# Sums of k v applied head by head, the tokens' root one list later, queries ahead of the last values, the last tile's layers in line

## The chip, the cores and the metric

The kernel runs on one core of one Trainium2 chip. The metric is the device time of one execution in microseconds (us), lower being better. Two kernels are compared by the medians of their runs. A profiled execution is one further execution, taken with the hardware profiler; its trace is what the profile's views are read from.

## What is computed

An input `x` of 256 channels by 64 by 64 positions (all float32) passes through two layers.

```python
# layer 0: x + conv(groupnorm(x)); 8 heads of 32 channels, each pixel a token
q, k = sigmoid(Wq x), sigmoid(Wk x);  v = (Wv x) / norm(v)
Ik  = integral(k)                      # running sums over rows and columns
Ikv = integral(k v^T)                  # a 32x32 matrix per head and pixel
for w in (1, 2, 4):                    # windows of 64, 32 and 16 pixels a side
    attn = q . box(Ikv, 64 // w)
    norm = q . box(Ik, 64 // w)
    outs.append(attn / (norm + 1e-6))
x = x + Wout concat(outs) + bout
# layer 1: 4096 tokens of 256
t = t + attention_ffn(layernorm(t))    # causal softmax, masked scores filled with -32767
t = t + experts(layernorm(t))          # top 2 of 8 experts, chosen once for all tokens
```

## The kernel before

It runs in three stages, one after the other on the same core: `window_attention` (to about 1031 us of the trace), `causal_attention` (to about 1771) and `experts`. TensorE (PE in the profile) does all products; its results land in PSUM and are evacuated by ScalarE (ACT) or VectorE (DVE). GpSimd is POOL, and SP and the other queues issue DMAs.

**The window stage.** `window_heads` runs twice, once for each half of the heads (hg = 0 and 1), so each call has four heads of 32 channels on the 128 partitions. Sums over a window are not taken from an integral image of `k v` at each pixel. They are split: keys near the window's edge are handled as masked scores (`push`: a mask product L348 and a score product L357 for each head, an evacuation with a maximum at zero L326 or L328, then `add`: the product with the values L390), and whole blocks of 8x8 pixels through `ikv`, the integral over blocks of the 32x32 sums of k v. For a row block Y (8 pixel rows) and each of the two smaller windows (`wi` = 1, 2), `states(Y)` forms with VectorE the 32x32 sums of the blocks that lie wholly inside (`srows` L487, `st8` L490 to L495) and spreads each into four block-diagonal matrices `bd`, one per head, in which the rows of the other heads are zero (eight copies on ScalarE, L498). `inside` then multiplies `bd` with `q` into the accumulator: for each of the 8 column blocks X and each head one product over all 128 partitions, L409. A float32 product shows as two matmul records.

Parts are packed into lists of up to 512 columns, and a loop over Y and over the lists i of Y (from L664) interleaves the rest: `spread_norms` at i = 1 (product L473, copies `rn` L476), the boxes of `ik` for the next Y on GpSimd at i = 2 (L440 to L453), the output product `convolve(Y - 1)` at i = 3 (L507, added to `t` at L512), and for hg = 1 `causal.norm(Y - 1)` at i = 4 and `causal.turn(Y - 1)` at i = 7. `norm` takes the statistics of four token tiles (L704, L705), the root of their variance (L709 on ScalarE) and its reciprocal (L710), and writes the four normalised tiles `xn` (L837); `turn` transposes them (L846). At Y = 7, `causal.load` puts the weights of attention into the memory of the integral image `ik`; three small buffers, `after`, `sums` and `count`, come from the same piece of memory.

**The order of the work.** In the window stage the orders of PE and POOL are written by hand: they follow the program's text. The orders of DVE, ACT and the DMA queues are made when the program is built, by a planner that forecasts when each instruction becomes ready; the program's text gives priorities. In `causal_attention` only PE's order is by hand. On each engine instructions run strictly in the order so made, and an instruction that waits holds all behind it.

**The attention stage.** The 32 query tiles of 128 tokens are taken from the last down, the 20 large ones (31 to 12) in turn, with the 12 small ones in between. `queries(g)` makes the queries of four tiles (L916, evacuated at L918), `scores` L956 with evacuation L958, row maximum L964 and exponential L969; `attend` transposes the weights (L986, copies `sT` L989) and multiplies with the values (L1000); `finish` L1010 to L1012. `causal.values(g)` makes four tiles of values (L856, evacuated at L858). Since masked scores count with a finite fill, the tokens behind a tile enter through `behind()`: running sums of `xs` (`sums`, filled first at L924, then 31 additions L926) times the value weights (L931), stored in `after` (L933). When four tiles are finished, `layers` queues six steps on the list `later`: first (L1040), turn (L1048, L1049), hidden (L1057, L1059), last (L1067 to L1075), norm (L1082), turn_again (L1090, L1091); `one()` takes one step from the list. The last group (tiles 12 to 15) does this for tiles 13 to 15 and then for tile 12 alone. `experts` begins with sums over all tokens, which need the last `turn_again`.

Of the kernel before, what the change touches and what calls it, by code (L numbers as in the profile page):

```python
# [177 lines left out]
def window_attention(tc, a, t, eps5, ident, causal, first):  # L178
# [5 lines left out]
    with ExitStack() as ctx:  # L184
# [99 lines left out]
        with tc.manual_schedule(engines={mybir.EngineType.PE}):  # L284
            causal.values(0, psum)
            for f in late:
                f()
            xns = causal.norm(7, w)
            causal.values(1, psum)
            causal.values(2, psum)  # L290
            causal.turn(7, xns, psum)


def window_heads(tc, a, t, ident, hg, norm, raws, load, psum, pools, tables, consts, late, causal):
# [109 lines left out]
    def inside(group, acc):  # L404

        wi, Y = group
        for X in range(8):
            for h, hs in enumerate(hss):
                nc.tensor.matmul(  # L409
                    acc.rearrange("p (y x) -> p y x", x=HW)[hs, :, 8 * X : 8 * X + 8],  # L410
                    lhsT=state["bd"][wi][:, X, h, :], rhs=q[:, 8 * Y : 8 * Y + 8, 8 * X : 8 * X + 8],
                    start=(X == 0), stop=False, skip_group_check=True,
                )

# [65 lines left out]
    def states(Y):  # L480


        out = [None]
        for wi in (1, 2):
            n = HALF[wi] // 8
            rows = state["h"].tile([P, 9, 32], F32, name="srows")
            nc.vector.tensor_sub(rows, ikv[:, min(8, Y + n), :, :], ikv[:, max(0, Y - n + 1), :, :])  # L487
            st = state["h"].tile([P, 8, 32], F32, name="st8")
            if n == 2:
                nc.vector.tensor_copy(st[:, 0, :], rows[:, 2, :])  # L490
                nc.vector.tensor_sub(st[:, 1:7, :], rows[:, 3:9, :], rows[:, 0:6, :])
                nc.vector.tensor_sub(st[:, 7, :], rows[:, 8, :], rows[:, 6, :])
            else:
                nc.vector.tensor_copy(st[:, 0:4, :], rows[:, 4:8, :])
                nc.vector.tensor_sub(st[:, 4:8, :], rows[:, 8:9, :].to_broadcast([P, 4, 32]), rows[:, 1:5, :])  # L495
            bd = state["h"].tile([P, 8, 4, 32], F32, name=f"bd{wi}")
            for h in range(4):
                nc.scalar.activation(bd[:, :, h, :], st, AF.Copy, scale=heads[:, 32 * h : 32 * h + 1])  # L498
            out.append(bd)
        return out  # L500

    def convolve(Y):
# [89 lines left out]
    with tc.manual_schedule(engines={mybir.EngineType.PE, mybir.EngineType.Pool}), ExitStack() as keys:  # L592
# [72 lines left out]
        for Y in range(8):  # L665
            ov = [None]
            for wi in (1, 2):
                o = h.tile([P, 8, HW], F32, name=f"ov{wi}")
                nc.sync.dma_start(out=o, in_=oscratch[wi].rearrange("b p (y x) -> y p b x", x=HW)[Y])
                ov.append(o)  # L670
            bd = states(Y)
            if hg and Y == 7:
                causal.load()
            for i, parts in enumerate(lists[Y]):
                if (Y, i) != (0, 0):
                    push(parts)
                if i == 2 and Y < 7:
                    boxed = boxes(Y + 1)
                if i == 1:
                    state.update(bd=bd, ov=ov, rn=spread_norms(r))  # L680
                if i == 3 and Y:
                    convolve(Y - 1)
                if hg and i == 4 and Y:
                    xns = causal.norm(Y - 1, w)
                if hg and i == 7 and Y:
                    causal.turn(Y - 1, xns, psum)
                if i == len(lists[Y]) - 3 and Y < 7:
                    r = norms(boxed)
# [87 lines left out]
class Causal:  # L776
# [23 lines left out]
    def load(self):  # L800
        nc, a = self.nc, self.a
        w = self.iks.tile([P, (HW + 1) * (HW + 1)], F32, name="ik")
        at = [0]

        def take(shape):
            n = int(np.prod(shape[1:]))
            s = w[0 : shape[0], at[0] : at[0] + n]
            at[0] += n
            return s.rearrange("p (c e) -> p c e", c=shape[1]) if len(shape) == 3 else s

        self.mm, self.mb, self.wvu, self.bvc = (take(d.shape) for d in self.fold)
        for i in (2, 3, 0, 1):
            nc.sync.dma_start(out=(self.mm, self.mb, self.wvu, self.bvc)[i], in_=self.fold[i])
        self.wt, self.col, self.row = {}, {}, {}
        for name in ("b1", "g_ln", "beta_ln"):
            s = self.col[name] = take([P, DC])
            nc.sync.dma_start(out=s, in_=a["L1_" + name].rearrange("(c p) -> p c", p=P))
        for name in ("W1", "W2"):
            s = self.wt[name] = take([P, DC, D])
            nc.sync.dma_start(out=s, in_=a["L1_" + name].rearrange("(c p) e -> p c e", p=P))  # L820
        for name in ("L1_b2", "L1_g_lnff", "L1_beta_lnff", "gamma", "beta"):
            s = self.row[name.removeprefix("L1_")] = take([P, D])
            nc.sync.dma_start(out=s, in_=a[name].partition_broadcast(P))
        self.after = take([NT, D + 1])
        self.sums = take([P, DC, NT])
        self.count = take([NT, 1])

    def norm(self, g, pool):
        nc = self.nc
        for i in range(4 * g, 4 * g + 4):  # L830
            statistics(nc, self.low, self.t[:, i, :], self.stats[:, i, :])
        rsqrt(nc, self.stats[:, 4 * g : 4 * g + 4, 1], self.eps5)
        xns = []
        for i, tag in enumerate(("l0Wq", "l0Wk", "l0Wv", "l0bo")):
# [26 lines left out]
class Given:  # L861
# [3 lines left out]
    def __init__(self, nc, a, pool, causal):  # L865
        def tile(name, shape, src=None):
            s = pool.tile(shape, F32, name=name)
            if src is not None:
# [14 lines left out]
        nc.gpsimd.memset(self.before, 1.0)  # L883
        nc.gpsimd.affine_select(out=self.before, in_=self.before, compare_op=ALU.is_gt, fill=0.0, base=0,
                                pattern=[[1, NE], [-1, NE]], channel_multiplier=0)
        self.stats = tile("stats2", [P, NT, 2])
        self.sums = tile("sums2", [P, DC, NQ + 1])
        self.parts = 0
# [2 lines left out]
def causal_attention(tc, t, ident, eps5, causal, big, given):  # L891
# [4 lines left out]
    with ExitStack() as ctx:  # L896
# [1 line left out]
        ps = ctx.enter_context(tc.tile_pool(name="l1ps", bufs=2, space=PSUM, reuse_waits="tile"))  # L898

        causal.rest(big)  # L900
        x, v, stats, after = causal.x, causal.v, causal.stats, causal.after
        mm, mb, wt, col, row = causal.mm, causal.mb, causal.wt, causal.col, causal.row
        x2 = {}
        for g in range(NQ):
# [15 lines left out]

        def behind():

            sums, count = causal.sums, causal.count
            nc.vector.memset(sums[:, :, NT - 1 :], 0.0)  # L924
            for i in reversed(range(NT - 1)):
                nc.vector.tensor_add(sums[:, :, i : i + 1], sums[:, :, i + 1 : i + 2], causal.xs[:, :, i + 1 : i + 2])  # L926
# [171 lines left out]
        with tc.manual_schedule(engines={mybir.EngineType.PE}):  # L1098
# [5 lines left out]
            def need(i):  # L1104
                if i // 4 not in qTs:
                    qTs[i // 4] = queries(i // 4)
# [3 lines left out]
                    later.pop(0)()  # L1110

            causal.values(3, value_psum)
            causal.values(7, value_psum)
            need(larges[0])
            for at, part in enumerate(scores(larges[0])):
                part()
                if at < 3:
# [3 lines left out]
            for r, i in enumerate(larges):  # L1121
# [7 lines left out]
                if r + 1 < len(larges):  # L1129
                    need(larges[r + 1])  # L1130
                    parts = scores(larges[r + 1])
                    for part in parts[:-1]:
                        part()
                    one()
                    todo.pop(0)()
                    parts[-1]()
                half = len(todo) // 2
                for step in todo[:half]:
                    step()
# [186 lines left out]
```

## Time and profile before

| | us |
|---|---|
| three runs | 2015.45, 2017.11, 2014.27 |
| median | 2015.45 |
| the profiled execution | 2017.58 |
| its span in the trace | 2015.9 |
| mean granted clock of PE | 0.977 of full speed |
| PE busy | 1862.9 |
| DVE, ACT, POOL busy | 985.5, 829.0, 431.2 |

The page's first part gives busy time, share of the span and the number of instructions for each engine; "PEld" is the loading of weights, which overlaps PE. A line of the timeline reads: start, duration, engine, source line, operation, what it writes `<-` what it reads, partitions and elements, how many instructions are merged in it, and in brackets the idle time of the engine before it and what ended that wait. In a line of a group by tile, the numbers behind the colon are the shortest, median and longest duration in ns, then the first and last start in us. A line under "who waited" is the idle time in us and the number of waits. In a table by stretches, a line reads: the stretch, its length, the busy time and the number of instructions of PE, PEld, DVE, ACT and POOL, then the granted clock of PE, the DMA share and the traffic in GB/s.

### The profile page before, as it was taken

How to read it: one execution, taken by the hardware profiler on the slowest of the kernel's cores; microseconds unless marked ns; L12 is line 12 of the kernel's file. 1: busy time of each engine (PE TensorE's matmuls, PEld its weight loads, DVE VectorE, ACT ScalarE, POOL GpSimd, SP SyncE). 2: the span in 40 equal slices, each digit the busy share in tenths (PEclk: the TensorE clock that was granted, in tenths of full speed). 3: DMA queues.
4: the chain of work that ended last, by engine and by line, in shares of the span. 5: the costliest groups of instructions: out<-in, count | busy, mean ns of one | idle time of the engine just before them, and what ended most of it. 6: DMA issues, size and time to landing. Idle time of an engine off the chain costs nothing.

```text
span 2015.9 us, 46364 instructions
## 1 busy us (share of the span) xinstructions
PE 1862.9 (92%) x20326; PEld 1224.0 (61%) x20326; DVE 985.5 (49%) x2190; ACT 829.0 (41%) x1459; POOL 431.2 (21%) x709
## 2 busy tenths in 40 slices
PE   4999899999999999898899999999999999879998
PEld 2655565555665565555574765666666666547787
DVE  4644444544554465555463434554554555433343
ACT  0566555554356654554413323332333233223322
POOL 1384322232155122333110000000000000021220
PEclk9999999999999999999999999999999999979999
DMA  7211000000331100000200000000000000010000
GB/s 239 80 52 50 23 13 16 15 18 13 96 98 40 44 18 13 18 13 12 49 2 0 0 1 0 1 1 0 1 0 1 0 1 0 1 42 21 21 21 21
DMA packets 66891, 53.35 MB, mean 26 GB/s; under 512 B 37568, under 2 KB 56792, under 8 KB 66688
## 3 DMA queue, kind: packets, MB, share of 16 engines
q1 hardware_dynamic: 57296, 31.87, 5.8%
q10 hardware_dynamic: 8128, 14.67, 2.1%
q0 software_dynamic: 1264, 3.84, 0.6%
q8 instruction: 159, 2.61, 0.5%
q14 instruction: 44, 0.36, 0.1%
HBM read 32.93 MB, written 17.44 MB: 25 GB/s over the span
## 4 chain that ended last, share of the span: by engine, by line
PE 42%; DVE 6%; ACT 3%; issue 2%; POOL 0%; ACTq 0%; DVEq 0%; POOLq 0%
PE po L1000 11%; PE pa L956 9%; PE ph L1260 6%; PE py L1280 5%; PE pt L986 2%; PE pm L1057 1%; PE acc L390 1%; PE pm L1067 1%; PE ps L357 1%; PE ps L507 1%; DVE lnst L704 1%; DVE sT L989 1%; DVE nbs L964 1%; PE pm L916 1%; ACT s L969 1%
## 5 line engine op out<-in xcount | busy, mean ns | idle before, releaser
L326 ACT ACTIVATE pm<-ps 128x512 f32<-128x512 f32 (+19 forms) x734 | 362.6, 559 | 320.3 <-issue 164.9
L328 DVE TENSOR_SCALAR pm<-ps 128x512 f32<-128x512 f32 (+23 forms) x442 | 267.8, 636 | 291.6 <-PE ps L357 210.8
L390 PE MATMUL acc<-pm,vh 128*32 128x248 f32 (+22 forms) x3424 | 220.1, 359 | 19.8 <-DVE pm L328 19.6
L357 PE MATMUL ps<-q,kh 32*128 32x248 f32 (+23 forms) x3424 | 209.8, 360 | 0.0
L956 PE MATMUL pa<-k,qT 128*128 128x512 f32 (+3 forms) x416 | 180.2, 574 | 7.1 <-ACT qT L918 5.7
L348 PE MATMUL ps<-table,table 32*128 32x192 bf16 (+19 forms) x2512 | 146.1, 262 | 39.3 <-DVE pm L328 18.4
L989 DVE COPY sT<-pt 128x512 f32<-128x512 f32 (+3 forms) x144 | 92.7, 643 | 138.1 <-PE pt L986 137.9
L348 PEld LDWEIGHTS <-table 32*128 32x128 bf16 x2512 | 51.0, 92 | 179.7 <-issue 172.8
L390 PEld LDWEIGHTS acc<-pm,vh 128*32 128x32 f32 x3424 | 88.9, 111 | 110.3 <-issue 63.2
L357 PEld LDWEIGHTS ps<-q,kh 32*128 32x128 f32 x3424 | 146.2, 192 | 7.5 <-issue 2.7
L425 POOL TENSOR_TENSOR y<-y,rn 128x512 f32<-128x512 f32 x32 | 40.8, 1275 | 477.5 <-DVE y L424 335.0
L958 ACT ACTIVATE s<-pa,v 128x512 f32<-128x512 f32 (+3 forms) x112 | 73.8, 662 | 148.6 <-PE pa L956 148.4
L956 PEld LDWEIGHTS pa<-k,qT 128*128 128x128 f32 x416 | 75.7, 191 | 89.3 <-issue 72.4
L964 DVE TENSOR_REDUCE nbs<-s 128x1 f32<-128x512 f32 (+4 forms) x120 | 77.6, 652 | 82.7 <-ACT s L958 58.9
L1280 PE MATMUL py<-w,hT 128*128 128x256 f32 x512 | 111.8, 379 | 0.0
L1000 PE MATMUL po<-kh,sT 128*128 128x257 f32 x406 | 101.3, 390 | 9.0 <-DVE sT L989 8.9
L1280 PEld LDWEIGHTS py<-w,hT 128*128 128x128 f32 x512 | 97.3, 190 | 15.7 <-issue 1.9
L390 PE MATMUL acc<-pm,v 128*32 128x192 f32 (+11 forms) x1600 | 98.5, 360 | 2.4 <-DVE pm L328 2.4
L357 PE MATMUL ps<-q,k 32*128 32x192 f32 (+11 forms) x1600 | 98.7, 359 | 0.7 <-issue 0.7
L1000 PEld LDWEIGHTS po<-kh,sT 128*128 128x128 f32 x406 | 73.7, 193 | 22.6 <-DVE sT L989 13.8
L507 PE MATMUL ps<-l0wo,y 128*128 128x256 f32 x384 | 87.2, 384 | 0.0
L947 POOL MEMSET s<- 128x32 f32 x20 | 2.5, 125 | 376.2 <-PE pt L986 348.4
(305 smaller groups left out, 2946.2 us busy)
## 6 DMA issues: line engine op xcount, KB each, us to landing
oscratch<-ov ACTq DMA_DIRECT2D x32, 256.0 KB
ov<-oscratch SPq DMA_DIRECT2D x32, 256.0 KB
t<-in_xT SPq DMA_DIRECT2D x32, 128.0 KB
vscratch<-v SPq DMA_DIRECT2D x32, 128.0 KB
vh<-vscratch SPq DMA_DIRECT2D x16, 256.0 KB
raw<-in_x ACTq DMA_DIRECT2D x7, 512.0 KB
raw<-in_x SPq DMA_DIRECT2D x7, 512.0 KB
out<-y SPq DMA_DIRECT2D x7, 512.0 KB
```

Source lines behind the costliest of these rows:

```text
L326: nc.scalar.activation(dst, src, AF.Relu)
L328: nc.vector.tensor_scalar_max(dst, src, 0.0)
L348: nc.tensor.matmul(got[h][:, spot].rearrange("p (y x) -> p y x", y=part.r1 - part.r0), lhsT=spread[hs, int(part.vertical), :], rhs=bias[hs ...
L357: nc.tensor.matmul(got[h][:, spot].rearrange("p (y x) -> p y x", y=part.r1 - part.r0), lhsT=keys[hs], rhs=q[hs, part.r0 : part.r1, part.c0 ...
L390: nc.tensor.matmul(out, lhsT=v, rhs=pm[:, h, spot].rearrange("p (y x) -> p y x", y=part.r1 - part.r0), start=fresh, stop=(left[key] == 0), ...
L507: nc.tensor.matmul(pt[:, i * D : (i + 1) * D], lhsT=ys[wi, Y][:, (2 * j + i) * P : (2 * j + i + 1) * P], rhs=wo[:, n, :], start=(n == 0), ...
L956: nc.tensor.matmul(pp[:, 0:m], lhsT=qTs[g][:, c, i * P - g * 512 : n - g * 512], rhs=x[b // 512][c][:, 0:m], start=(c == 0), stop=(c == DC ...
L964: nc.vector.tensor_reduce(nbs[:, at : at + 1], s[:, b : b + m], AX.X, ALU.max)
L989: nc.vector.tensor_copy(sT[:, 0:full], pt[:, 0:full])
L1000: nc.tensor.matmul(acc, lhsT=sT[0:m, j * P : (j + 1) * P], rhs=rhs, start=(b == 0), stop=(m != P))
L1260: nc.tensor.matmul(ph, lhsT=w1v[:, e, c, f, :], rhs=x2[g][c], start=(c == 0), stop=(c == DC - 1))
L1280: nc.tensor.matmul(py, lhsT=hT[:, e, f, j * P : (j + 1) * P], rhs=w2v[:, e, f, :], start=(e + f == 0), stop=(e == 1 and f == FC - 1))
```

## The change

Four edits, and what goes with them:

1. `causal.norm` is split. `measure` holds the statistics and stays at i = 4; root, reciprocal and `xn` move to i = 5. For the last row block, `measure(7)` is called immediately ahead of `norm(7)`.
2. `inside` multiplies each head's 32 partitions of `st` with the same 32 partitions of `q`, instead of all 128 partitions of `bd` with all of `q`. The copies to `bd` are gone; `st` gets a buffer for each window (`st1`, `st2`) in place of the shared `st8`.
3. `after` moves out of the memory of `ik` into a tile of the pool that is kept to the end; `sums` and `count` become tiles of attention's small pool. The first queries are made ahead of `values(7)` instead of behind it.
4. For the last large tile, each step of `attend` is followed by one step of `later`.

```diff
@@ window_attention
             for f in late:
                 f()
+            causal.measure(7)
             xns = causal.norm(7, w)
@@ inside
-                    lhsT=state["bd"][wi][:, X, h, :], rhs=q[:, 8 * Y : 8 * Y + 8, 8 * X : 8 * X + 8],
+                    lhsT=state["st"][wi][hs, X, :], rhs=q[hs, 8 * Y : 8 * Y + 8, 8 * X : 8 * X + 8],
@@ states
-            st = state["h"].tile([P, 8, 32], F32, name="st8")
+            st = state["h"].tile([P, 8, 32], F32, name=f"st{wi}")
...
-            bd = state["h"].tile([P, 8, 4, 32], F32, name=f"bd{wi}")
-            for h in range(4):
-                nc.scalar.activation(bd[:, :, h, :], st, AF.Copy, scale=heads[:, 32 * h : 32 * h + 1])
-            out.append(bd)
+            out.append(st)
@@ the loop over Y in window_heads
-            bd = states(Y)
+            st = states(Y)
...
-                    state.update(bd=bd, ov=ov, rn=spread_norms(r))
+                    state.update(st=st, ov=ov, rn=spread_norms(r))
...
                 if hg and i == 4 and Y:
+                    causal.measure(Y - 1)
+                if hg and i == 5 and Y:
                     xns = causal.norm(Y - 1, w)
@@ Causal
-        self.after = take([NT, D + 1])
-        self.sums = take([P, DC, NT])
-        self.count = take([NT, 1])
+
+    def measure(self, g):
+        for i in range(4 * g, 4 * g + 4):
+            statistics(self.nc, self.low, self.t[:, i, :], self.stats[:, i, :])
 
     def norm(self, g, pool):
         nc = self.nc
-        for i in range(4 * g, 4 * g + 4):
-            statistics(nc, self.low, self.t[:, i, :], self.stats[:, i, :])
@@ Given
+        self.after = tile("after", [NT, D + 1])
@@ causal_attention
-        x, v, stats, after = causal.x, causal.v, causal.stats, causal.after
+        x, v, stats, after = causal.x, causal.v, causal.stats, given.after
@@ behind
-            sums, count = causal.sums, causal.count
+            sums = sm.tile([P, DC, NT], F32, name="behind", bufs=1)
+            count = sm.tile([NT, 1], F32, name="count", bufs=1)
@@ the end of causal_attention
             causal.values(3, value_psum)
+            need(larges[0])
             causal.values(7, value_psum)
-            need(larges[0])
...
+                if r == len(larges) - 1:
+                    while todo:
+                        todo.pop(0)()
+                        one()
                 half = len(todo) // 2
```

## The prediction

> **What bounds the kernel now.** I read the page first, then the idle gaps of the matmul engine in order of time, then the timeline around each large gap that an edit touches, and last the granted clock there. The page says who sets the pace:
>
> ```profile
> PE 1862.9 (92%) x20326; PEld 1224.0 (61%) x20326; DVE 985.5 (49%) x2190; ACT 829.0 (41%) x1459; POOL 431.2 (21%) x709
> ```
>
> PE is never far from busy, so a change is worth what it takes from PE's own work or from its gaps. Added up over the trace, gaps above 60 ns come to 119.9 us. Five places matter here. First, Y=6 of the second head group:
>
> ```profile
> 953.14 0.28 PE L348 MATMUL ps<-table,table 32*128 32x248 bf16 x3
> ...
> 957.90 1.19 POOL L440 TENSOR_TENSOR rows<-ik 128x520 f32<-128x520 f32 x1
> ...
> 959.16 0.06 DVE L924 MEMSET ik<- 128x2 f32 x1 [9.82 <-POOL rows L440]
> 959.24 1.14 DVE L328 TENSOR_SCALAR pm<-ps 128x440 f32<-128x440 f32 x2
> ...
> 959.90 0.36 PE L348 MATMUL ps<-table,table 32*128 32x248 bf16 x4 [6.48 <-DVE pm L328]
> ```
>
> The reader is to see that VectorE stood 9.82 us at a fill of two elements a partition. That fill belongs to `behind()` (L924), which the program calls a stage later; its first product, L931, runs at 1081.07. Its target lies in the tile `ik`, so it must wait until GpSimd has read `ik` for the last time (L440). The planner had put it ahead of two evacuations, and PE waited 6.48 us for them. The next stretch then ran at half clock:
>
> ```profile
> 960.00:964.00 4.00, 4.00 (x38) 2.54 (x38) 0.98 (x2) 1.38 (x3) 1.48 (x3) 0.50 0.73 177
> ```
>
> Second, the first row block of each head group (207 to 216, again 693 to 701):
>
> ```profile
> 208.57 0.46 DVE L487 TENSOR_TENSOR srows<-ikv 128x288 f32<-128x288 f32 x1 [2.61 <-DMA oscratch<-ov]
> ...
> 210.09 1.71 ACT L498 ACTIVATE bd<-st,heads 128x256 f32<-128x256 f32 x4 [1.86 <-DVE st L492]
> ...
> 211.70 1.04 ACT L476 COPY rn<-ps 128x512 f32<-128x512 f32 x2
> ...
> 212.32 0.33 PE L348 MATMUL ps<-table,table 32*128 32x168 bf16 x8 [2.47 <-ACT rn L476]
> ```
>
> Here four `bd` copies stand on ScalarE ahead of the norms' copies `rn`, which hold PSUM that PE wants. Third, the tokens' norms in the second head group:
>
> ```profile
> 866.83 0.30 ACT L709 ACTIVATE stats<-stats,eps 128x4 f32<-128x4 f32 x1 [6.57 <-DVE stats L705]
> ...
> 867.38 1.38 DVE L837 TENSOR_SCALAR xn<-t,stats 128x256 f32<-128x256 f32 x4
> 868.67 1.28 DVE L328 TENSOR_SCALAR pm<-ps 128x509 f32<-128x509 f32 x2
> 869.41 0.39 PE L348 MATMUL ps<-table,table 32*128 32x93 bf16 x9 [1.55 <-DVE pm L328]
> ```
>
> Root, reciprocal and four `xn` run before evacuations (L326, L328) that the program writes earlier. So the planner issues whatever is ready in its own forecast; place in the text only breaks ties. The fill at 959.16 says the same. Fourth, the products with `bd` and what waits for the copies:
>
> ```profile
> L409 PE MATMUL acc<-q,bd x2048: 217/219/316, 221.7 to 1024.6; 128*32 128x64 f32 x187
> L498 ACT ACTIVATE bd<-st,heads x128: 492/493/516, 210.1 to 989.4; 128x256 f32<-128x256 f32 x128
> DVE st L494: 25.7, 16
> DVE st L490: 17.3, 10
> ```
>
> Fifth, the end of attention:
>
> ```profile
> 1750.90 2.43 PE L1067 MATMUL pm<-ik,hT 128*128 128x256 f32 x10 [0.24 <-ACT hT L1059]
> 1759.58 1.67 PE L1090 MATMUL pt<-ident,att 128*128 128x128 f32 x6 [6.24 <-DVE att L1082]
> 1770.32 0.69 PE L1090 MATMUL pt<-ident,att 128*128 128x128 f32 x2 [4.03 <-DVE att L1082]
> ```
>
> **What the Trainium skill says.** "TensorEngine Tiling (Array Packing)", Key Properties: a change of tiling mode drains TensorE. The trace agrees and prices it. I took the start of the first product after a change of line, less the time at which the columns of the one before had streamed: L390 to L409 (both 128x32) 18 ns early in the median of 30, L409 to L390 17 ns early (32), but L357 (32x128) to L390 91 ns late (290) and L390 to L348 98 ns late (237). A change of form costs about 113 ns more than none. "TensorE: Matmul & The Clock Gate", Part 3, says that small tiles in distinct row and column groups run together; L586 (64x32) agrees, eight starts 6 to 7 ns apart, while no 32x32 tile is in this trace. The tiling page, Gotcha 1, warns that different row tiles cannot access the same PSUM bank at once. In this kernel L348, L357 and L586 give each row group its own bank, so no run shows the case. The clock page, Part 1, says that an idle matmul engine loses half its clock; the window above has 0.50 after the 6.48 us gap.
>
> **Part by part.** Minus is a gain.
>
> *Sums, count and `after` out of the `ik` tile.* The fill no longer touches `ik`. Its new tile is in attention's small pool, laid out behind `qT`, `s` and `nbs`; adding up the pools' sizes, this falls on a buffer of `pm`, whose last reader is PE's L390 at the end of the window stage. A fill held there waits for PE, which isn't late in itself. Gone: the gap of 6.48. At half clock the same list and the next convolution took 959.90 to 963.48 (3.58) and 5.73, against 243.85 to 246.00 (2.15, three products more) and 5.45; I take 1.5 of that. The count's iota on GpSimd (0.13 at 960.09) moves too, beside nothing that waits. The loads on SP (L813 to L823) keep waiting for `ik`, used 70 us later. Sum -8.0; from -6.5 to -9.
>
> *Products head by head.* Removed: 128 `bd` copies, 54.9 us of ScalarE, nearly all beside PE. They cost where they stand ahead of `rn`: from L473 to the resumed L348 it is 207.62 to 212.32 (4.70) and 693.00 to 697.67 (4.67), against 1.79 at Y=1 (240.16 to 241.95). That is 2.9 each; should the DMA wait of `srows` remain, 2.5 each, since VectorE's evacuation still ends at 209.6. I take -5.2 (from -5 to -5.8). Following half clock: 212.32 to 220.13 is 7.81 against 4.73 for the same two lists (251.38 to 256.11), and 697.67 to 701.40 is 3.73 against 2.13, so 2.9 without its small gap and 1.6; I take -3.5 (from 0 to -4.5). VectorE no longer stands 25.7 + 17.3 us for ScalarE. Instead `st` itself waits for the old products; with evacuations queued behind it, it can wait about what ScalarE waited for them, 8.3 us. Small PE gaps at such places (0.39, 0.31, 0.56, 0.77, 0.33) sum to 2.4; I take -1.0 (from 0 to -2.4). Added: each call's 64 records are 16 groups of four, 55.6 ns apart, 0.89 us. With 32 rows they stream as many columns, so the same 0.89, but the form changes going in and coming out: 2 x 0.113 x 32 calls = +7.2, on PE and hidden by nothing. Bounds 0 (if the 32x32 drain were free) and the rival below. Sum -2.5.
>
> *Root one list later.* `measure` stays where the statistics were, so root and `xn` become ready at the same moment; by the third view they are issued when ready. I take 0. Bounds: 0 and the rival's -9.6.
>
> *Queries ahead.* They fill PE while VectorE evacuates values. The gaps there are 0.67 (three waits at L856 for `v`) and under 0.5 before the second score product (1061.23). I take -0.5 (from 0 to -1). The bias of tile 31 now comes right before its use, 0.43 us of VectorE; two score buffers cover that.
>
> *Last tile in line.* PE work is unchanged. L1067 of the three tiles came at 1750.07; put ahead of the last two steps of attention (1744.3 to 1747.4) it starts 3.1 sooner, and three small waits of PE there (0.35, 0.44, 0.24) mostly go, say 0.9. But the L1048 ahead of it now waits for `att` (1739.83 onward) with only four transposes beside it, by estimate 1.5 more. The chain L1069 to L1082 (7.4 us) then shares VectorE with `sT` copies and the last `finish`, about 1.3 of those rows. -3.1 - 0.9 + 1.5 + 1.3 = -1.2; from +1 to -3.
>
> Sum: -8.0 - 2.5 + 0 - 0.5 - 1.2 = -12.2. The profiled execution took 2017.6 (span 2015.9 and 1.7 around it), so 2005.4 on its scale. It lies 2.1 above the median of the three runs, 2015.45, and I forecast on the median: **2003.3 us**.
>
> **Rivals.** *The root really moves* (chance 0.13). Seven norms cost PE gaps of 10.6 (four of 1.87, one of 1.90, two of 0.61), against 0.22 each at the same place without a norm: 9.1. Half clock after two of them: 2.5. Root, reciprocal and `xn` then delay the next list: 2.0 back. -9.6 more: 1993.7. Against it: the order the third view shows. *The stall comes back* (0.20): another instruction of attention, ready in the plan but not on the chip, takes the fill's place on VectorE or ScalarE. 8.0 of the gain is lost: 2011.3, near no change. For it: the planner has no guard. Against: the new tile's last user is PE. *Slower: the four diagonal tiles don't run together in one bank* (0.15). Two at a time makes a call 1.78 instead of 0.89, +28.5: 2031.8; one at a time 3.56, +85: 2088. It decides once a call's products exceed 1.27 us, as 12.2 / 32 = 0.38. For: Gotcha 1. Against: the tiles write different partitions, and column tiles share a bank today (L409, L390) at full rate.
>
> **How the numbers follow.** The forecast has 0.52. Its own range adds the terms' distances to their bounds as root of the sum of squares: 7.8 down (mostly the change of form being free), 4.5 up (mostly half clock staying), so 1995.5 to 2007.8. The range 1993 to 2013 takes in the root and the returned stall and leaves out the slower case and a little at the ends. Within 0.2% (2011.4 to 2019.5), about what a measurement of this kernel tells from no change, lie half of the returned stall and an end of the forecast: 0.13. Slower 0.16, faster 0.71.
>
> **What would show it.** No wait of VectorE on GpSimd near 950, and no PE gap of 6 us there. L473 to L348 under 2 us at Y=0. Product calls of 0.89 us with a start about 95 ns late on both sides; a call over 1.2 us would make the prediction wrong. Root, reciprocal and `xn` in the old place, with five gaps near 1.55. L1090 of three tiles about a microsecond sooner.

## The result, and the profile after

| | before | after |
|---|---|---|
| median of four runs on one chip, us | 2016.28 | 1993.84 |
| lowest and highest | 2014.27 to 2018.01 | 1988.91 to 1994.53 |
| the profiled execution | 2017.58 | 1994.53 |
| its span | 2015.9 | 1992.8 |
| mean granted clock of PE | 0.977 | 0.982 |
| PE gaps above 60 ns behind its first product, summed | 119.9 | 100.9 |

The ratio of the times is 0.9884, with a 95% interval of 0.9865 to 0.9903: 23.4 us faster (19.6 to 27.2), where 12.2 had been forecast. The direction was right and the size was half of what came. Line numbers of after lie up to 5 away from those of before: L327 and L329 are the evacuations, L349 the mask products, L358 the scores, L391 the products with the values, L410 the products with `st`, L477 `rn`, L488 `srows`.

The page's line of busy times, after:

```profile
PE 1859.6 (93%) x20326; PEld 1218.4 (61%) x20326; DVE 1000.5 (50%) x2190; ACT 777.4 (39%) x1331; POOL 431.8 (22%) x709
```

ScalarE has lost its 128 copies (54.9 us; its busy time fell by 51.6). PE has the same products, busy for 3.3 us less. So the gain lies in PE's gaps (19.0 us less) and in its clock. The fill that had held VectorE for 9.82 us in front of two evacuations now comes when the window stage is over (from the group of the tile `behind`):

```profile
L925 DVE MEMSET behind<- x1: 60/60/60, 1018.6 to 1018.6; 128x2 f32 x1
```

In the first row block of the first head group, the timeline after shows that `srows` waits for nothing and no copy stands ahead of `rn`:

```profile
204.32 0.46 DVE L488 TENSOR_TENSOR srows<-ikv 128x288 f32<-128x288 f32 x1
...
206.06 1.13 PE L474 MATMUL ps<-r,spreadh 32*128 32x512 f32 x6
...
207.27 1.57 ACT L477 COPY rn<-ps 128x512 f32<-128x512 f32 x3 [0.60 <-PE ps L474]
...
207.91 0.33 PE L349 MATMUL ps<-table,table 32*128 32x168 bf16 x8 [0.22 <-ACT rn L477]
```

From L474 to the resumed L349 it is 1.85 us instead of 4.70. The norms of the second head group stand where they stood, in the timeline of the same block as before:

```profile
853.98 0.30 ACT L709 ACTIVATE stats<-stats,eps 128x4 f32<-128x4 f32 x1 [6.57 <-DVE stats L705]
...
854.53 1.38 DVE L836 TENSOR_SCALAR xn<-t,stats 128x256 f32<-128x256 f32 x4
855.82 1.28 DVE L329 TENSOR_SCALAR pm<-ps 128x509 f32<-128x509 f32 x2
856.56 0.38 PE L349 MATMUL ps<-table,table 32*128 32x93 bf16 x9 [1.55 <-DVE pm L329]
```

The same 6.57 of waiting, the same order, the same gap of 1.55: the edit to the root did nothing.

To see where time went I cut both traces at the same events of PE, whose order is by hand and (but for the end of attention) the same: each row block runs from its first `spread_norms` product to that of the next. "Lost clock" is the time by which the trace's clock records fall short of full clock, summed over the stretch. In the row blocks these records show full clock or half, and half clock for 3.41 us or a multiple of it, so that a block loses 0, 1.71, 3.41 or 5.12 us of clock.

| stretch | before: us, PE gaps, lost clock | after |
|---|---|---|
| head group 0, Y=0 | 32.54, 4.99, 3.41 | 26.25, 1.30, 0.00 |
| head group 0, Y=1 | 36.35, 2.44, 0.00 | 35.93, 1.73, 0.00 |
| head group 0, Y=3 | 42.53, 3.00, 0.00 | 43.87, 2.33, 1.71 |
| head group 0, Y=4 | 43.56, 2.61, 0.00 | 44.09, 2.74, 0.00 |
| head group 0, Y=5 | 44.88, 3.26, 0.00 | 44.58, 2.60, 0.00 |
| head group 1, Y=0 | 30.87, 4.58, 1.71 | 26.26, 1.30, 0.00 |
| head group 1, Y=6 | 50.33, 9.60, 5.12 | 40.69, 2.96, 0.00 |
| first scores to the experts | 712.12, 40.99, 11.63 | 712.46, 39.61, 13.44 |

Row blocks repeat to about 0.02 us from execution to execution where full clock is granted (head group 0, Y=1, takes 36.35 to 36.36 in before, memory_alone, root_alone and srows_free), so they show effects that a median of runs can't. Where half clock falls differs between executions, as the row of Y=3 shows: shorter gaps, and yet a longer block.

### The profile page after: what moved, and what is told of

Read it like the earlier page. It is cut to its first block, busy times and chain, and to the rows that moved or that the text cites. A ratio compares the mean times of both kernels' runs of the same rounds, so it can differ in the third digit from the quotient of the medians.

```text
span 1992.8 us, 46271 instructions
## 1 busy us (share of the span) xinstructions
PE 1859.6 (93%) x20326; PEld 1218.4 (61%) x20326; DVE 1000.5 (50%) x2190; ACT 777.4 (39%) x1331; POOL 431.8 (22%) x709
## 3 DMA queue, kind: packets, MB, share of 16 engines
q8 instruction: 159, 2.61, 0.6%
## 4 chain that ended last, share of the span: by engine, by line
PE 42%; DVE 6%; ACT 3%; issue 1%; POOL 0%; ACTq 0%; DVEq 0%; POOLq 0%
PE po L1001 11%; PE pa L957 10%; PE ph L1265 6%; PE py L1285 6%; PE pt L987 2%; PE pm L1058 1%; PE acc L391 1%; PE pm L1068 1%; DVE lnst L704 1%; PE ps L505 1%; DVE sT L990 1%; PE ps L358 1%; DVE nbs L965 1%; PE pm L916 1%; ACT s L970 1%
## 5 line engine op out<-in xcount | busy, mean ns | idle before, releaser
L327 ACT ACTIVATE pm<-ps 128x512 f32<-128x512 f32 (+19 forms) x734 | 362.4, 558 | 348.4 <-issue 194.1
L329 DVE TENSOR_SCALAR pm<-ps 128x512 f32<-128x512 f32 (+23 forms) x442 | 267.6, 636 | 315.7 <-PE ps L358 234.5
L391 PE MATMUL acc<-pm,vh 128*32 128x248 f32 (+22 forms) x3424 | 218.5, 356 | 16.8 <-DVE pm L329 16.7
L358 PE MATMUL ps<-q,kh 32*128 32x248 f32 (+23 forms) x3424 | 204.8, 354 | 0.0
L349 PE MATMUL ps<-table,table 32*128 32x192 bf16 (+19 forms) x2512 | 143.1, 261 | 24.4 <-ACT rn L477 8.4
L391 PEld LDWEIGHTS acc<-pm,vh 128*32 128x32 f32 x3424 | 87.3, 110 | 108.5 <-issue 60.8
L349 PEld LDWEIGHTS <-table 32*128 32x128 bf16 x2512 | 50.0, 92 | 162.5 <-issue 155.7
L358 PEld LDWEIGHTS ps<-q,kh 32*128 32x128 f32 x3424 | 142.6, 188 | 7.3 <-issue 2.5
L426 POOL TENSOR_TENSOR y<-y,rn 128x512 f32<-128x512 f32 x32 | 41.3, 1290 | 449.5 <-DVE y L425 297.9
L391 PE MATMUL acc<-pm,v 128*32 128x192 f32 (+11 forms) x1600 | 98.5, 360 | 3.9 <-DVE pm L329 2.4
L358 PE MATMUL ps<-q,k 32*128 32x192 f32 (+11 forms) x1600 | 98.4, 359 | 0.0
```

Source lines behind the costliest of these rows:

```text
L327: nc.scalar.activation(dst, src, AF.Relu)
L329: nc.vector.tensor_scalar_max(dst, src, 0.0)
L349: nc.tensor.matmul(got[h][:, spot].rearrange("p (y x) -> p y x", y=part.r1 - part.r0), lhsT=spread[hs, int(part.vertical), :], rhs=bias[hs ...
L358: nc.tensor.matmul(got[h][:, spot].rearrange("p (y x) -> p y x", y=part.r1 - part.r0), lhsT=keys[hs], rhs=q[hs, part.r0 : part.r1, part.c0 ...
L391: nc.tensor.matmul(out, lhsT=v, rhs=pm[:, h, spot].rearrange("p (y x) -> p y x", y=part.r1 - part.r0), start=fresh, stop=(left[key] == 0), ...
```

## The experiments

Fourteen kernels, each measured against before on the same chip; intervals are 95%. "Edit" is against the kernel that the expectation names.

**memory_alone.** Edit: the three buffers out of `ik`, as in the change, in before.

```diff
-        self.after = take([NT, D + 1])
-        self.sums = take([P, DC, NT])
-        self.count = take([NT, 1])
+        self.after = tile("after", [NT, D + 1])
...
+            sums = sm.tile([P, DC, NT], F32, name="behind", bufs=1)
+            count = sm.tile([NT, 1], F32, name="count", bufs=1)
...
```

> The kernel before, with only the move of sums, count and after out of the memory of ik. Theory A (the move removes the one stall and the half clock behind it, nothing else): 8.6 us faster than before (7.5 to 10), a PE gap of 6.5 us gone near 953. Theory B (the record's sum was right here and wrong nowhere else, so the rest of the 22 comes from edits acting together): the same 8, so this run alone doesn't tell A from B; it does tell both from theory C (another instruction takes the fill's place on VectorE when the other edits aren't there): 0 to 1 us faster.

2006.19 us, ratio 0.9961 (0.9949 to 0.9974): 7.9 us faster (5.2 to 10.3). The block Y=6 of head group 1 takes 41.63 instead of 50.33, its gaps 3.11 instead of 9.60 (1.71 of lost clock is left there, where after has none). Nothing takes the fill's place; C is out.

**products_alone.** Edit: `st` head by head and no `bd`, in before (the line of the product).

```diff
-                    lhsT=state["bd"][wi][:, X, h, :], rhs=q[:, ...]
+                    lhsT=state["st"][wi][hs, X, :], rhs=q[hs, ...]
```

> The kernel before, with only the products head by head (no copies bd, st of its own for each window). Theory A (ScalarE freed of the copies starts the norms' r and rn sooner at every row block, and the record took this too small): 12 us faster than before (10 to 15), with the PE gaps behind the reciprocals 0.67 us shorter each and the half clock of both first row blocks gone. Theory B (the record's terms hold, and the missing 10 us come from somewhere else): 2.5 us faster (0 to 5).

2003.76 us, ratio 0.9951 (0.9933 to 0.9970): 9.9 us faster (6.0 to 13.5). B is out: the prediction's -2.5 was mis-sized. Both first row blocks take 26.26, and six other blocks have 0.65 to 0.70 less of gaps each. In four of them it is the gap behind the reciprocals, as A said; in the other two (Y=1 and Y=5 of head group 0) gaps of 0.56 and 0.77 are gone that the prediction had listed. The gain is a little under A's 10 to 15.

**root_alone.** Edit: `measure` split off, `norm` at i = 5, in before.

> The kernel before, with only measure split from norm and norm called one list later. Theory A (the planner issues root, reciprocal and xn when the statistics are ready, wherever the text has them): no change, within 1 us, the five PE gaps of 1.55 behind xn still there. Rival (the root moves and frees the evacuations): 9.6 us faster, these gaps gone.

2013.49 us, ratio 0.9999 (0.9984 to 1.0013). No change; the rival is out.

**full_height.** Edit, in after:

```diff
-                    lhsT=state["st"][wi][hs, X, :], rhs=q[hs, ...]
+                    lhsT=state["st"][wi][:, X, :], rhs=q[:, ...]
```

> The kernel after, but the products with st over all 128 partitions of st and q, so the tile form stays 128x32 as before, without copies. Each head's sum then takes in the other heads' rows, so the outputs are not the reference's; numbers of products and columns are the same. Theory A (the change of tile form costs 0.22 us a call and nothing hides it): 7 us faster than after (5.5 to 8.5). Rival (the drain lies where PE would have waited for evacuations anyway): 0 to 3 us faster than after.

1981.74 us, ratio 0.9837 (0.9816 to 0.9857). Against after that is 9.5 us by the ratios, on different chips and uncertain by 5.6. The stretches are sharper: in the eight row blocks with full clock in both it is 0.40 to 0.54 us shorter than after, 0.485 in the mean, and there are two calls in a block: 0.24 us a call, 7.8 in all 32. The start times say the same: in after the first L410 starts 112 ns later behind L391 than the first L409 behind L390 in before, and the L391 behind the call 108 ns later (medians of 30 and 32 calls); the call itself is 0.02 us longer. In full_height both delays are gone. The change of form is paid in full; A holds.

**copies_kept.** Edit, in after: `bd` is filled by its four copies as before, and `st` is used.

```diff
+            bd = state["h"].tile([P, 8, 4, 32], F32, name=f"bd{wi}")
+            for h in range(4):
+                nc.scalar.activation(bd[:, :, h, :], st, AF.Copy, scale=heads[:, 32 * h : 32 * h + 1])
             out.append(st)
```

> The kernel after, with the copies to bd issued again in their old place though nothing reads them (same memory for bd as before; the products stay head by head on st). Theory A (it is ScalarE's queue: the copies stand ahead of the norms' r and rn at every row block): 14 us slower than after (10 to 18), PE gaps behind the reciprocals 0.67 us longer again, the first row blocks of both head groups at about 31 us instead of 26.3. Theory B (the copies cost only in the first row blocks, as the record had it): 8.7 us slower, no longer gaps elsewhere. Theory C (what helped is that the products no longer wait for copies, not ScalarE's queue): within 2 us of after.

2021.18 us, ratio 1.0036 (1.0022 to 1.0050): slower even than before, by its trace 25 us behind after. A's direction holds and C is out; B's 8.7 is far too small; but A's size and place fail too. The gap behind the reciprocals in Y=2 of head group 0 grew from 1.22 to 1.52, not to 1.89, and most of the other added gaps are PE waiting for ScalarE's evacuations (12.1 us in 41 waits, after 5.2 in 21) and for `rn` (16.2 in 16 waits, after 8.4). All gaps are 16.3 longer, and 11.9 more of clock is lost. Copies that nothing reads don't wait for the old products, so they stand elsewhere than in before: this kernel shows that ScalarE's queue matters, not what it cost in before.

**root_delayed.** Edit, in after, in part: real edges. `issue_after` makes what the block issues queue behind the given instruction on its engine.

```diff
-                if hg and i == 5 and Y:
-                    xns = causal.norm(Y - 1, w)
+                if hg and i in (5, 6) and Y:
+                    with tc.issue_after(state["ev", 0]), tc.issue_after(state["ev", 1]):
+                        if i == 5:
+                            causal.root(Y - 1)
+                        xns = (xns if i == 6 else []) + causal.norm(Y - 1, w, range(2 * i - 10, 2 * i - 8))
```

> The kernel after, with edges that really hold the root and the reciprocal behind the last evacuations of list 5, two of the xn behind those of list 5 and two behind those of list 6. Theory A (the five gaps of 1.55 and two of about 0.3 come only from root, reciprocal and xn standing ahead of an evacuation on VectorE): 7.5 us faster than after (5 to 10), gaps gone. Rival (VectorE has no room anywhere in these lists, so that the same wait shows one or two lists later, or in the turn at list 7): within 2 us of after, with new PE gaps for VectorE or for the transposes of xn.

1977.32 us, ratio 0.9819 (0.9806 to 0.9832): 13 us below after by the ratios, 15.2 by the spans (of which 2.4 is clock in attention, where nothing was edited). The same block in its timeline:

```profile
849.09 1.26 DVE L330 TENSOR_SCALAR pm<-ps 128x509 f32<-128x509 f32 x2
849.50 0.69 PE L350 MATMUL ps<-table,table 32*128 32x93 bf16 x12
...
852.97 0.18 DVE L714 RECIPROCAL stats<-stats 128x4 f32<-128x4 f32 x1 [0.99 <-ACT stats L713]
853.19 0.74 DVE L843 TENSOR_SCALAR xn<-t,stats 128x256 f32<-128x256 f32 x2
...
854.75 0.40 DVE L843 TENSOR_SCALAR xn<-t,stats 128x256 f32<-128x256 f32 x1
```

The evacuations run first, L350 follows without a gap, and the `xn` fill VectorE's idle time two lists later. PE's waits for VectorE at this line fall from 8.2 to 0.6 us, all gaps from 100.9 to 91.6. A's mechanism is shown. Its 7.5 was too small: the gaps alone gave 9.3. The rest is clock: 0.984 to 0.987 in its five runs, 0.982 to 0.984 in after's four.

**both_alone.** Edit: memory_alone and products_alone together, in before.

> The kernel before, with the memory move and the products head by head, and none of the rest (root, order of the queries, last tile). Theory A (the two make the whole change; the rest is worth about nothing): 22 us faster than before (20 to 24), the same as after within 1.5 us. Theory B (the two add up to the 17.8 that they gave apart, and the rest gives the other 4): 18 us faster.

1992.72 us, ratio 0.9888 (0.9873 to 0.9903): 22.6 us (19.5 to 25.6), after's own gain. A holds: these two edits are the change. That they gave 17.8 apart doesn't contradict it, since the two intervals make that sum uncertain by 4.5 (root of the sum of squares of 2.6 and 3.7); whether the two also help each other, these runs can't tell.

**hoisted.** Edit, in `add` of after:

```diff
         parts, spots, pm = waiting.pop(0)
+        ahead = [part for part in parts if part.key not in accs and not part.vertical and part.wi]
+        if ahead:
+            accs[ahead[0].key] = po.tile([P, 512], F32, name="acc")
+            inside(ahead[0].group, accs[ahead[0].key])
```

> The kernel after, with the products of a new group made at the start of the list in which the group begins, between the score products (32x128) and the first product with the values (128x32), instead of in the midst of the products with the values. That saves one of the two changes of tile form of each of the 30 calls that aren't first already. Theory A (each change of form costs 0.11 us on the path, whatever the forms): 3.4 us faster than after (2.5 to 4.5). Rival (a change from 32x128 to 32x32 costs as much more, or the accumulator isn't free yet, so that PE waits): 0, or slower by some 5.

1988.58 us, ratio 0.9872 (0.9857 to 0.9887): too near to after for the runs to tell. The eight row blocks with full clock in both are 0.26 to 0.28 shorter each, which makes 4.3 us if it holds in all sixteen. A holds.

**copies_behind.** Edit, in before, in part: `bd` as before, but its copies, and a `st` for each window, behind the last `rn`.

```diff
+        with tc.issue_after(state["last"]):
+            for wi in (1, 2):
...
+                    nc.scalar.activation(bd[:, :, h, :], sts[wi], AF.Copy, scale=heads[:, 32 * h : 32 * h + 1])
```

> The kernel before, with the copies to bd kept and still used by the products over 128 partitions, but held by edges on ScalarE behind the last rn copy of the same row block (st of its own for each window). Theory A (not ScalarE's load costs, but the place of the copies ahead of r and rn): 15 us faster than before (11 to 18), both first row blocks at about 25.5 us instead of 31 to 32.5. Rival (the copies cost wherever they stand, since evacuations or the products with bd queue behind them): within 4 us of before.

2072.12 us, ratio 1.0287 (1.0272 to 1.0302): both theories fail. The group of the tile `st`, under "who waited":

```profile
DVE st L490: 48.0, 13
```

The next block's `st` has to wait for the late copies of this one's, on VectorE, with evacuations behind it. At Y=1 VectorE stands 3.98 us and PE 3.52. Holding one queue back moved the stall to another; the run says nothing on the copies' cost.

**room_kept.** Edit, in `states` of after:

```diff
+            if Y == 0:
+                bd = state["h"].tile([P, 8, 4, 32], F32, name=f"bd{wi}")
+                nc.gpsimd.memset(bd[:, 0, 0, 0:2], 0.0)
             out.append(st)
```

> The kernel after, with tiles of the size of bd kept in the window stage's memory (two elements of each filled once by GpSimd in the first row block), nothing copied. Theory A (part of the gain in the first row blocks is memory: with bd gone, srows no longer shares memory with the tiles ov that a transfer still reads): the wait of 2.61 for that transfer is back ahead of the first srows, and each first row block takes 0.8 to 1.5 us more than in after, together 2 us slower. Rival (memory plays no part): both first row blocks as in after, 26.3 us.

2002.47 us, ratio 0.9949 (0.9930 to 0.9968). The first row blocks took 30.98 and 30.86, nearly what they took before: far more than A's 1.5. But the trace shows a fault of the experiment. The fill waited 36.70 us for PE with GpSimd's boxes behind it, so the boxes ran beside VectorE's `st`:

```profile
208.33 0.50 DVE L488 TENSOR_TENSOR srows<-ikv 128x288 f32<-128x288 f32 x1 [2.61 <-DMA oscratch<-ov]
...
212.55 1.47 DVE L488 TENSOR_TENSOR srows<-ikv 128x288 f32<-128x288 f32 x1
...
214.66 0.37 PE L349 MATMUL ps<-table,table 32*128 32x93 bf16 x9 [2.92 <-DVE pm L329]
```

**tail_later.** Edit, at the end of attention in after:

```diff
                 if r == len(larges) - 1:
+                    todo.pop(0)()
+                    todo.pop(0)()
                     while todo:
```

> The kernel after, with the last large tile's first two steps of attend run without a step of layers between them, so that the first transposes of the normalised tiles come two steps later. Theory A (the edit at the end gave nothing because PE met att too soon, 2.4 us, and went on at half clock, 1.5 us): the 2.42 in front of these transposes gone, the eight products behind them at 2.0 us instead of 3.5, the later wait for att longer than 3.45; in sum 2 us faster than after (0.5 to 3.5). Rival (the chain over VectorE at the end sets the time whatever PE does): within 0.5 us, the later wait back at 6 us or more.

1990.77 us, ratio 0.9877 (0.9855 to 0.9898); from the first scores to the experts 711.30 instead of 712.46, 1.2 us, within A's range (up to the last tile both lose the same clock; the runs can't tell the two kernels apart). The 2.42 is gone and the eight products take 2.00 again, as A said, but the wait for `att` is back at 6.36, as the rival said. Most of what PE saves there it waits later.

**together.** Edit: root_delayed, hoisted and tail_later in one, in after.

> The kernel after, with the root held back (as in root_delayed), the products of a new group at the start of its list (as in hoisted) and the last tile's steps as in tail_later. Theory A (three separate costs on PE's path): 16 + 4 + 2 = 22 us faster than after, 2.2% below it, some 1972 us (1968 to 1976). Rival (with less slack on PE one of the waits comes back): no better than root_delayed, 1977 or more.

1973.11 us, ratio 0.9799 (0.9785 to 0.9813): 40 us below before, and 17 below after by the ratios, where 22 had been expected (the expectation's 2.2% would be against before). The stretches show that the three act side by side: blocks with full clock are 0.27 shorter than in root_delayed (Y=1, 4 and 6 of head group 1), as in hoisted, and the wait for `att` is 6.36, as in tail_later. It has the lowest median of the study, though its interval overlaps that of root_delayed.

**room_late.** Edit: as room_kept, with `if Y == 7`.

> The kernel after, with tiles of the size of bd kept in the window stage's memory as in room_kept, but filled by GpSimd (two elements each) only in the last row block, so that GpSimd's boxes aren't held up in the first. srows shares memory with ov again, no copies. Theory A (the transfer's wait is most of the gain in the first row blocks): each first row block near 31 us, 9 us slower than after. Theory B (the wait by itself costs its 0.8, and room_kept's further gap of 2.92 came from GpSimd working beside VectorE): each first row block at 27 to 28 us, 2 us slower than after.

1994.89 us, ratio 0.9898 (0.9871 to 0.9924). First row blocks 26.81 and 26.79, a little under B's 27. The wait is there and costs PE its 0.78, as B said and not A:

```profile
208.76 0.46 DVE L488 TENSOR_TENSOR srows<-ikv 128x288 f32<-128x288 f32 x1 [2.60 <-DMA oscratch<-ov]
...
209.79 0.38 PE L349 MATMUL ps<-table,table 32*128 32x168 bf16 x9 [0.78 <-DVE pm L329]
```

**srows_free.** Edit, in before: the tile `bd` is taken one step earlier, so that it, not `srows`, lies on the memory of `ov`.

```diff
+            bd = state["h"].tile([P, 8, 4, 32], F32, name=f"bd{wi}")
             rows = state["h"].tile([P, 9, 32], F32, name="srows")
...
-            bd = state["h"].tile([P, 8, 4, 32], F32, name=f"bd{wi}")
```

> The kernel before, with the tile bd taken ahead of srows, so that bd lies where srows lay: srows no longer shares memory with ov, copies and products stay. Theory A (the wait of VectorE for the transfer is most of the cost in the first row blocks): each first row block at 26 to 27 us, 9 us faster than before. Theory B (wait and copies together: the copies stand ahead of rn all the same): PE still waits 2 us or more for rn, each first row block at 29 to 30.5 us, 2 to 4 us faster than before.

2010.70 us, ratio 0.9980 (0.9970 to 0.9990): 4.0 us faster (2.0 to 6.0). First row blocks 29.34 and 29.32, with full clock. The copies still stand ahead of `rn`:

```profile
208.27 1.70 ACT L498 ACTIVATE bd<-st,heads 128x256 f32<-128x256 f32 x4 [0.31 <-DMA oscratch<-ov]
209.88 1.04 ACT L476 COPY rn<-ps 128x512 f32<-128x512 f32 x2
...
210.49 0.33 PE L348 MATMUL ps<-table,table 32*128 32x168 bf16 x8 [1.94 <-ACT rn L476]
```

B holds. The four combinations for a first row block (two head groups), which settle what room_kept had left open:

| us | transfer's wait | no wait |
|---|---|---|
| copies | 32.54, 30.87 (before) | 29.34, 29.32 |
| no copies | 26.81, 26.79 | 26.25, 26.26 (after) |

The two kernels without copies carry 0.5 of changed form. So without the wait the copies cost 29.33 - 26.26 + 0.5 = 3.6; the wait by itself costs 0.54; and where both meet, half clock followed in all six first row blocks traced (before, memory_alone, root_alone), while with one of the two alone it did not (srows_free, room_late).

## Why the prediction was right and wrong

The prediction's terms beside what the traces of before and after give:

| term | predicted | measured | from |
|---|---|---|---|
| fill out of `ik` | -8.0 | -10.1 | block Y=6: 50.33 to 40.69, and the 0.49 that the form costs there |
| first row blocks | -8.7 | -11.9 | 32.54 and 30.87 to 26.25 and 26.26, and 0.95 of form |
| small gaps elsewhere | -1.0 | -4.1 | PE gaps of Y=1 to 6 (5 in the second group) |
| change of form | +7.2 | +7.8 | full_height |
| root | 0 | 0 | root_alone |
| queries ahead | -0.5 | -0.1 | 10.69 to 10.55 |
| last tile in line | -1.2 | +0.3 | 712.12 to 712.46 |
| sum | -12.2 | -18.1 | |

The spans differ by 23.1. Of the 5.0 left, 1.6 lies ahead of the first row block, and 3.2 in two stretches (from Y=7 of head group 0 to the next group, and Y=7 of head group 1; 0.49 of form added to each) in which the profiled execution of before lost 5.1 us of clock more. In other kernels this clock comes and goes: the last stretch lost 1.71 in memory_alone, root_alone, full_height and room_late, and nothing in products_alone and after. That makes it chance in this pair of executions. But the medians of the runs also differ by more than 18.1 (19.6 to 27.2), so some of the rest must be the change's own; where, the runs do not show.

**Right.** The fill, with its mechanism and its place; the root at 0, against the rival whose total, 1993.7, is nearly the measured time. A total that fits isn't a mechanism: the seven gaps are all still there, and root_alone changed nothing. The change of form, and with it the four diagonal tiles: the 64 records of a call start within 0.88 us (before 0.86), four of them 6 to 7 ns apart. The stalls that would have come back (2011.3) and the slow tiles (2031.8) did not come.

**Wrong: the step "Products head by head".** It was put at -2.5. By the table it gave -11.9 - 4.1 + 7.8 = -8.2, and products_alone measured 9.9 (6.0 to 13.5). Its +7.2 was right; what the copies cost was put too small, in three places.

First, "Small PE gaps at such places ... sum to 2.4; I take -1.0". Those gaps all went, 1.7 of them in Y=1 to 6. But I had looked for the copies only ahead of `rn`. They stood directly ahead of the norms' `r` too, in ten of its sixteen, and `r` starts four reciprocals on VectorE, 3.38 us, with the evacuation behind them that PE waits for. The timeline of before:

```profile
307.87 0.89 ACT L498 ACTIVATE bd<-st,heads 128x256 f32<-128x256 f32 x2
...
308.67 0.66 ACT L464 ACTIVATE r<-ps,eps 96x512 f32<-96x512 f32 x1
...
309.75 3.38 DVE L466 RECIPROCAL r<-r 96x128 f32<-96x128 f32 x4
...
313.72 0.31 PE L390 MATMUL acc<-pm,vh 128*32 128x64 f32 x4 [1.89 <-DVE pm L328]
```

And of after:

```profile
299.48 1.03 PE L462 MATMUL ps<-box,sums 128*32 128x512 f32 x6
...
300.62 0.68 ACT L465 ACTIVATE r<-ps,eps 96x512 f32<-96x512 f32 x1 [1.55 <-PE ps L462]
...
301.34 3.38 DVE L467 RECIPROCAL r<-r 96x128 f32<-96x128 f32 x4 [0.21 <-ACT r L465]
...
305.31 0.31 PE L391 MATMUL acc<-pm,vh 128*32 128x64 f32 x4 [1.22 <-DVE pm L329]
```

`r` now follows its product at once, and PE's gap is 0.67 shorter. Four gaps shrank so and four others by 0.13; four with no copies ahead of `r` grew by some 0.1. The waits summed by pair showed these gaps as VectorE's evacuations (22.0 us in 20 waits), never as ScalarE's copies, and I didn't follow that chain back. The prediction's upper bound of 2.4 was thus too small, not only the value taken.

Second, the other gaps of the first row blocks. The gap ahead of the resumed L348 was nearly right: from the first L474 it is 2.8 shorter in both blocks, put at 2.6. But all gaps of the two blocks are 7.0 shorter, not 5.2. srows_free shows how the copies reach further: they cost 3.6 in a block, of which 1.3 lies ahead of the resumed L348 (3.15 there against 1.85 in after). And "should the DMA wait of `srows` remain" was treated as an either-or. It went as well (with `bd` gone, `srows` no longer lies on memory of `ov`); alone it costs 0.54, with the copies it brought half clock.

Third, half clock, and here the fill's term fell short too. The prediction had 1.5 for the fill and 3.5 for the first row blocks. What these blocks gained beyond their gaps and the form is 3.5 and 4.9. They lost 5.12, 3.41 and 1.71 of clock, and in after all of that is gone. I had priced only the stretch right behind each gap. Some of that is luck: in five of the ten other traces without the stall (memory_alone and both_alone among them) Y=6 still loses 1.71. In the Trainium skill, "TensorE: Matmul & The Clock Gate", Part 1, says that the window which judges how busy the engine is runs freely, so that the same gaps can meet it at different phases. The runs agree: head group 0, Y=2, takes 44.02 in after with 1.71 of lost clock and 42.40 in room_late with none, at the same 2.33 of gaps.

**Wrong in the other direction: the last tile.** The -1.2 counted 1.5 for PE waiting for `att`. It is 2.42, and the products behind it run near half clock (0.53). The timeline of after:

```profile
1716.58 1.67 PE L1049 MATMUL pt<-ident,att 128*128 128x128 f32 x6 [2.42 <-DVE att L1041]
...
1719.29 3.52 PE L1001 MATMUL po<-kh,sT 128*128 128x257 f32 x8
...
1736.77 1.67 PE L1091 MATMUL pt<-ident,att 128*128 128x128 f32 x6 [3.45 <-DVE att L1083]
```

The wait at L1091 is 2.8 shorter, as meant; the new wait, and 1.5 more for eight products that take 2.00 in both_alone, use it up: over the stage PE's gaps are 1.4 less, and 1.8 more of clock is lost.

## What to carry to other kernels

A copy in a queue costs what stands behind it, and through that what stands behind *that*: follow a wait for one engine's evacuation back through the engine's own queue, block by block, before setting a bound on it. Where a planner orders an engine by readiness, a later place in the program may move nothing, so check in the trace whether a moved step moved, and use a real edge if it must (here worth 13 us). Gaps of a few microseconds are to be priced with the clock that they cost behind them, and that clock is to be looked up in several executions, since it comes and goes.

## What the runs showed of the hardware

- A change of tile form between 128x32 and 32x32 cost 0.24 us a call, both ways together, on the path. The order of forms can save one change: where the 32x32 products came straight behind the 32x128 ones, a call was 0.13 us cheaper (hoisted).
- Four 32x32 tiles on the diagonal, writing four groups of partitions of one bank, ran at nearly the pace of four 128x32 tiles: 0.88 us against 0.86 for 64 records. The Trainium skill's "TensorEngine Tiling (Array Packing)", Gotcha 1, warns of row tiles in one bank; for tiles that write different partitions, each with its own rows, no such limit showed.
- Half clock in the row blocks came for 3.41 us or a multiple, and at equal gaps in some executions and not in others. One such piece, 1.71 us of lost clock, made a block 1.6 us longer (head group 0, Y=2: 44.02 in after, 42.40 in room_late).
- A VectorE subtraction of 128x288 took 0.46 us alone. Where 1.1 us of it lay beside a GpSimd product of 128x512, it took 1.41 in after (four times, beside L426) and 1.40 and 1.47 in room_kept (beside L454).
- A new tile on memory that a transfer still read held VectorE for 2.61 us (before); laid elsewhere, it did not wait (after, srows_free).
